# Four graph layers on one core: rounded-type mask transposes, and attention stacks by way of DRAM

## The chip, the cores and the metric

The kernel runs on one core of a Trainium2 chip. A core has a matrix engine (TensorE, PE in profiles; its weight loads are shown as PEld), three other compute engines (VectorE or DVE, ScalarE or ACT, GpSimd or POOL), a queue engine that only starts transfers here (SyncE, SP), and sixteen DMA engines. Data lie in DRAM, in the on-chip SBUF with 128 partitions, or in PSUM, into which TensorE writes. The metric is the device time of one execution in microseconds, lower is better. Three executions of the kernel before took 4090.72, 4092.49 and 4097.2 us; the median is 4092.49.

## What is computed

The input is `x` (16 graphs, 1024 nodes, 256 features) and one adjacency matrix `adj` of 1024 x 1024 integers, the same for all graphs. Four layers follow, each as `x = x + layer(relu(layernorm(x)))`. Three are graph attention layers, with 4, 1 and 1 heads; the fourth is a transformer block with 8 heads of 32 features:

```python
h = jnp.maximum(_layernorm(x, axis=-1), 0.0)
x = x + _L0_gnn_ref(h, adj, L0_gnn_W, L0_gnn_a)     # 4 heads of 64, then elu
...
# within a graph layer (L1 of them; L0 and L2 differ in heads and slopes)
h = jnp.matmul(inp, W)
e = jax.nn.leaky_relu(e_src[:, :, None] + e_dst[:, None, :], negative_slope=ALPHA)
e = jnp.where(adj[None, :, :] == 0, NEG_INF, e)
attention = jax.nn.softmax(e, axis=-1)
h_prime = jnp.matmul(attention, h)
...
# within the fourth layer
scores = jnp.einsum('fnhd,fmhd->fhnm', q, k) / jnp.sqrt(jnp.asarray(D, x.dtype))
scores = jnp.where(mask, scores, jnp.asarray(-1000000000.0, x.dtype))
attn = jax.nn.softmax(scores, axis=-1)
t = jnp.einsum('fhnm,fmhd->fnhd', attn, v).reshape(F, N, C)
x = _layernorm(x + t, ln1_g, ln1_b)
h = jax.nn.relu(jnp.einsum('fnc,cd->fnd', x, w1) + b1)
f_out = jnp.einsum('fnd,dc->fnc', h, w2) + b2
x = _layernorm(x + f_out, ln2_g, ln2_b)
```

## The kernel before

**Tiles.** A graph is eight row tiles of 128 nodes. `P` is 128, `HALF` is 512 nodes (half a graph), `TH` is 4 tiles in a half, `HG` is 4 heads in a group. The adjacency is turned once into `mask`, a byte array with the source node on partitions, which all graphs and all layers use.

**An order planned by hand.** The function `direct` emits nothing at first. It records every operation as a `Work` with an engine, an estimated duration, the buffers it reads and writes, and a rank (`rec.stream`, `KNOTS`, `LEAD`, `priority`). `Record.schedule` (L189) then plays the whole program through a model of five queues: `pe`, `act`, `dve`, `pool`, and `dma`, which is SyncE. It takes at each moment the work with the smallest rank that is ready, and emits the instructions in that order. `PASS` is the delay that it assumes before another engine can use a result; `SWITCH` times `BIAS` is the price of turning TensorE from one kind of matmul to another; `moved` and `lands` are the assumed transfer time and landing delay of a DMA; `AHEAD` and `SLACK` shape how long SyncE is held and how late a transfer is counted as there. The order on each engine is then fixed: on the chip an engine waits at an instruction whose input is late, and everything behind it waits too.

**Start.** `setup` (L661) prepares the weights of the first graph layer, then calls `neighbours` (L617) for each of the eight row blocks of `adj`. It loads 512 KB into `a32` (L621), DVE compares it with zero into `nat` (L626), TensorE turns eight 128 x 128 blocks with `transposes` (L526, instruction at L529), ACT casts them from PSUM into `mask` (L644), and DVE takes the smallest entry of each row into `least` (L653). `a32` and `nat` are both taken from the ring `r_pa` of six buffers. The layer 0 work of graphs 0 and 1 runs side by side at the start, the second in buffers lent from later stages (`lent`).

**Graph layers.** `gat` (L725): normalise (L500), transpose, project (L770), spread a row of scores over all partitions by a DRAM copy (`turn_rows` L843 writes `rd`, `spread` L852 reads it back as `row`), form weights on DVE (L868), multiply on TensorE. With four heads the products are L982 and the sums L992, in 32-column pieces; with one head it is L895.

**Attention.** For each graph, `attention` (L1082) makes keys and queries in `project` (L1125): TensorE multiplies (L1132), ACT casts to the rounded type into `hi` (L1141), DVE takes the rest into `lo` (L1144). Score matmuls in the rounded type then need a *stack* of 128 partitions for each head: four times the 32 features, as hi, hi, lo, lo for queries and hi, lo, hi, lo for keys. Sixteen transfers from SBUF to SBUF (L1154), one for each of four parts and four heads, put it together. `hi` and `lo` have one buffer each, the key stack `r_ks` one of [4, 1024], the query stack `r_qs` two of [4, 512]. There are eight such projections for each graph, 128 in all. The steps that follow are scores (L1352), exponential (L1376), mask (L1385), products (L1217); `later` places the other projections between them. For most graphs GpSimd adds weights up by accumulating transfers (L1253).

**End.** `feed` (L1398) does the two products of the transformer block (L1449), loads the rest of the sum `xr` from DRAM (L1502) and writes the output (L1574). After all planned work, a few instructions fold four checks of the value range into `flag` (L1661 to L1674); where a check fails, the slow function `general` computes everything again (L2227).

Of the kernel before, what the change touches and what calls it, by code (L numbers as in the profile page):

```python
# [22 lines left out]
P = 128  # L23
# [90 lines left out]


WEIGHT = {"pe": 1.0, "dve": 0.3}
PASS = {"pe": 0.198, "act": 0.153, "dve": 0.202, "pool": 0.13, "dma": 0.0}


class Work:  # L120
# [23 lines left out]
class Record:  # L144
# [44 lines left out]
    def schedule(self):  # L189
        for n, x in enumerate(self.work):  # L190
            x.n = n
            if x.key is None:
                x.key = priority(x)
            x.left = len(x.before)
            for y in x.before:
                y.after.append(x)
        free = dict.fromkeys(PASS, 0.0)
        queue = 0.0
        future = {e: [] for e in PASS}
        now = {e: [] for e in PASS}  # L200
        mode = "full"
        for x in self.work:
            if not x.left:
                heapq.heappush(future[x.engine], (x.ready, x.n, x))

        def opening(x):

            at, need = 0.0, {}
            for buf in x.opens:
                need[buf.ring] = need.get(buf.ring, 0) + 1  # L210
            for ring, n in need.items():
                if len(ring.free) < n:
                    return None
                at = max(at, sorted(ring.free)[n - 1][0])
            return at

        def turn(x):

            return BIAS * SWITCH.get((mode, x.modes[0]), 0.0) if x.engine == "pe" else 0.0

        def choose(e):

            at = free[e]
            while future[e] and future[e][0][0] <= at:
                x = heapq.heappop(future[e])[2]
                heapq.heappush(now[e], (x.key, x.n, x))
            best = None
            for key, n, x in now[e]:
                t = opening(x)
                if t is not None:  # L230
                    best = min(best or (1e9,), (max(at, t), key + turn(x), n, x))
            if future[e] and (best is None or future[e][0][0] < best[0]):
                for t, n, x in sorted(future[e]):
                    if opening(x) is not None:
                        t = max(t, at, opening(x))
                        best = min(best or (1e9,), (t, x.key + turn(x), n, x))
                        break
            return best

        order = []  # L240
        while True:
            choices = [(c, e) for c, e in ((choose(e), e) for e in PASS) if c]
            if not choices:
                break
            (at, _, n, x), e = min(choices, key=lambda c: c[0][0])
            if (x.key, n, x) in now[e]:
                now[e].remove((x.key, n, x))
                heapq.heapify(now[e])
            else:
                future[e].remove((x.ready, n, x))  # L250
                heapq.heapify(future[e])
            for buf in x.opens:
                _, k = heapq.heappop(buf.ring.free)
                buf.k, buf.t = k, buf.ring.tiles[k]
            us = x.us
            if e == "pe":
                us += SWITCH.get((mode, x.modes[0]), 0.0)
                mode = x.modes[1]
            x.start = at
            if x.moved:  # L260
                queue = max(at + (us if e == "pool" else 0.2), queue) + x.moved
                us = max(us, queue - at - AHEAD)
                x.pass_on = queue + x.lands + SLACK - (at + us)
            order.append(x)
            free[e] = at + us
            for buf in x.shared:
                buf.end = max(buf.end, at + us + x.pass_on)
                buf.uses.remove(x)
                if not buf.uses:
                    heapq.heappush(buf.ring.free, (buf.end, buf.k))  # L270
            for y in x.after:
                y.ready = max(y.ready, at + us + (x.pass_on if y.before[x] else 0.0))
# [10 lines left out]
KNOTS = {  # L283
    "gat0": (-6.706, -3.534, -2.307, -1.522, -2.815),
    "gat1": (0.005, 0.503, 0.618, 0.731, 0.916),
    "gat2": (0.938, 0.468, 0.637, 0.867, 1.15),
    "beside": (0.241, 1.203, 1.943, 0.54, 4.121),
    "values": (1.06, -3.362, -0.305, 3.145, 0.767),
    "steps": (1.014, 1.448, 1.59, 2.064, 1.794),
    "feed": (2.016, 2.165, 2.509, 2.154, 2.609),  # L290
    "last": (2.808, 3.335, 3.547, 5.206, 6.138),
}
BIAS = 1.225
LEAD = {"act": 9.55, "dve": -0.732}

SWITCH = {
    ("full", "col4"): 0.137,
# [30 lines left out]
def direct(ctx, tc, flag, x, adj, gat_w, gat_a, w_qkv, ln1_g, ln1_b, ln2_g, ln2_b, w1, b1, w2, b2, out):  # L328
# [33 lines left out]
    mask = const.tile([P, NT, N], U8, name="mask")  # L362

    least = const.tile([P, NT], F32, name="least")


    work = ctx.enter_context(tc.tile_pool(name="work", bufs=1))
# [53 lines left out]
    def act(us, emit, w, r):  # L421
        rec.add("act", us, emit, w, r)
# [100 lines left out]
            [b_rec],  # L523
        )

    def transposes(dst, src, n, shape=P):  # L526

        for k in range(n):
            nc.tensor.transpose(dst(k), src(k), ident[:shape, :shape])  # L529

    class Halves:

# [81 lines left out]
                [],  # L614
            )

    def neighbours(it):  # L617
        a32, nat = r_pa.new(), r_pa.new()
        a_i = a32.t.rearrange("p a n -> p (a n)").bitcast(I32)
        dma(  # L620
            1.8, 1.7, lambda: nc.sync.dma_start(a_i, adj[it * P : (it + 1) * P, :]), [a32], []  # L621
        )
        nat_f = nat.t.rearrange("p a n -> p (a n)")
        dve(
            ts_us(N),
            lambda: nc.vector.tensor_scalar(nat_f, a_i, 0.0, None, ALU.is_gt),  # L626
            [nat],
            [a32],
        )
        for j0 in range(0, NT, TH):  # L630
# [1 line left out]
            pe(  # L632
                0.109 * TH,
                lambda: transposes(
                    lambda k: g.t[:, k * P : (k + 1) * P],
                    lambda k: nat_f[:, (j0 + k) * P : (j0 + k + 1) * P],
                    TH,
                ),
                [g],
                [nat],  # L640
            )
            act(
                act_us(HALF),
# [11 lines left out]
            [a32],  # L655
        )

    def mask_of(hf):
# [423 lines left out]
    def attention(b, xt, b_mv, b_rstd):  # L1082
# [42 lines left out]
        def project(g, hf, keys, stack, at):  # L1125
# [4 lines left out]
            def product():  # L1130
# [14 lines left out]
                [lo],  # L1145
                [sc, hi],
            )
            for a in range(4):
                part = ((hi, hi, lo, lo), (hi, lo, hi, lo))[keys][a]
                for r in range(HG):  # L1150
                    dma(
                        0.3,
                        1.5,
                        lambda: nc.sync.dma_start(  # L1154
                            stack.t[a * D3 : (a + 1) * D3, r, at : at + HALF],
                            part.t[r * D3 : (r + 1) * D3, :],
                        ),
                        [stack((r, hf if keys else 0, a))],
                        [part],
                        us=0.59,  # L1160
                    )

        def values(it):
            sc = r_sc.new()
# [501 lines left out]
    good = work.tile([P, 4], F32, name="good")  # L1666
# [4 lines left out]
    nc.tensor.matmul(ps[:1, :4], ones_col, good, start=True, stop=True)  # L1671
    n_good = work.tile([1, 1], F32, name="n_good")
    nc.vector.tensor_reduce(n_good, ps[:1, :4], AX.X, ALU.add)
    nc.vector.tensor_scalar(flag, n_good, 4.0 * P - 0.5, None, ALU.is_lt)  # L1674


@with_exitstack
# [590 lines left out]
```

## Time and profile before

| | |
|---|---|
| median of three executions | 4092.49 us |
| the profiled execution | 4091.28 us, of which the span from first to last instruction is 4089.5 us |
| mean granted TensorE clock | 0.995 |
| mask transposes (L529, from `pa`) | 64 of 128 x 128, 10.9 us busy |
| score matmuls (L1352) | 2048, 717.7 us busy, mean 455 ns |
| stack transfers (L1154) | 2048 of 64 KB on SyncE's queue |
| row spreads (L852) | 184 of 256 KB on the same queue |
| accumulating transfers (L1253) | 240 of 512 KB on GpSimd's queue, median 6.0 us from issue to landing |
| all DMA traffic | 389.65 MB, of which the queue that SyncE feeds 259.36 MB (22.4% of the 16 engines' span) |

The profile is one execution, its times in microseconds from the first instruction. "PE" times overlap: matmuls are pipelined, so a mean duration of one is longer than the time between two. An arrow "<-" in a wait names the instruction that released it; in a group of instructions it stands between output and inputs.

### The profile page before, as it was taken

How to read it: one execution, taken by the hardware profiler on the slowest of the kernel's cores; microseconds unless marked ns; L12 is line 12 of the kernel's file. 1: busy time of each engine (PE TensorE's matmuls, PEld its weight loads, DVE VectorE, ACT ScalarE, POOL GpSimd, SP SyncE). 2: the span in 40 equal slices, each digit the busy share in tenths (PEclk: the TensorE clock that was granted, in tenths of full speed). 3: DMA queues.
4: the chain of work that ended last, by engine and by line, in shares of the span. 5: the costliest groups of instructions: out<-in, count | busy, mean ns of one | idle time of the engine just before them, and what ended most of it. 6: DMA issues, size and time to landing. Idle time of an engine off the chain costs nothing.

```text
span 4089.5 us, 68377 instructions
## 1 busy us (share of the span) xinstructions
PE 4023.3 (98%) x23874; PEld 2354.7 (58%) x23874; DVE 3499.0 (86%) x5994; ACT 2689.9 (66%) x6673; POOL 646.7 (16%) x631
## 2 busy tenths in 40 slices
PE   7999999999999999999999999999999999999998
PEld 3566466564655646566564665646556465665643
DVE  7768898988979799897988989889797998979866
ACT  5467676775757767576675767757577675765765
POOL 1102011121211202111121211212111011111100
PEclk9999999999999999999999999999999999999999
DMA  3024344343444324443243443434443244432441
GB/s 128 24 77 102 99 109 99 89 93 98 101 112 102 90 75 112 114 108 90 77 105 99 109 105 87 95 92 103 110 109 85 74 112 113 108 90 59 107 103 47
DMA packets 215248, 389.65 MB, mean 95 GB/s; under 512 B 45168, under 2 KB 80240, under 8 KB 214896
## 3 DMA queue, kind: packets, MB, share of 16 engines
q1 hardware_dynamic: 180336, 259.36, 22.4%
q0 software_dynamic: 34560, 125.84, 16.2%
q8 instruction: 191, 3.13, 0.3%
q14 instruction: 161, 1.32, 0.1%
HBM read 91.03 MB, written 33.95 MB: 31 GB/s over the span
## 4 chain that ended last, share of the span: by engine, by line
PE 85%; DVE 5%; ACT 4%; SPq 2%; DMA 2%; issue 1%; POOL 1%; DVEq 0%; ACTq 0%; POOLq 0%
PE bank L895 20%; PE bank L1217 14%; PE sc L1352 11%; PE bank L982 9%; PE bank L770 9%; PE bank L529 6%; PE bank L992 5%; PE bank L1449 4%; PE sc L1132 4%; PE sc L1169 2%; SPq L1154 2%; DVE pt L868 2%; DVE pa L1385 1%; POOL rstdz L466 1%; ACT waste L446 1%
## 5 line engine op out<-in xcount | busy, mean ns | idle before, releaser
L1385 DVE TENSOR_TENSOR pa<-pa,mask 128x1024 f32<-128x1024 f32 x1024 | 1221.4, 1218 | 72.4 <-ACT pa L1376 69.4
L1376 ACT ACTIVATE pa<-sc 128x512 f32<-128x512 f32 x2048 | 1098.3, 606 | 234.2 <-PE sc L1352 175.1
L868 DVE SCALAR_TENSOR_TENSOR pt<-row,e,mask 128x512 f32<-128x512 f32 x1472 | 1016.3, 744 | 62.2 <-DMA row<-rd 40.3
L895 PE MATMUL bank<-qb,pt 128*128 128x257 f32 x4096 | 942.0, 380 | 3.5 <-ACT fz L1533 3.5
L895 PEld LDWEIGHTS bank<-qb,pt 128*128 128x128 f32 x4096 | 771.3, 189 | 147.1 <-ACT pa L1376 12.6
L1352 PE MATMUL sc<-qs,ks 128*128 128x512 f32 x2048 | 717.7, 455 | 11.2 <-DMA qs<-lo 5.8
L1217 PE MATMUL bank<-pa,va 128*32 128x512 f32 x4096 | 504.8, 596 | 0.3 <-DVE pa L1385 0.2
L1352 PEld LDWEIGHTS sc<-qs,ks 128*128 128x128 f32 x2048 | 360.4, 189 | 212.3 <-ACT pa L1376 56.5
L1244 DVE TENSOR_TENSOR sums<-pa,pa 128x1024 f32<-128x1024 f32 x360 | 430.3, 1219 | 57.6 <-PE bank L1217 57.4
L982 PE MATMUL bank<-pt,qb 128*32 128x512 f32 x3840 | 468.7, 597 | 2.4 <-DVE pt L868 1.4
L770 PE MATMUL bank<-w_aug,hT 128*128 128x259 f32 (+1 forms) x1504 | 383.1, 393 | 0.5 <-ACT hT L764 0.5
L1253 POOL DMA_DIRECT2D sums<-pa x240 | 210.1, 878 | 930.5 <-DVE pa L1385 507.2
L770 PEld LDWEIGHTS bank<-w_aug,hT 128*128 128x128 f32 x1504 | 275.8, 191 | 121.1 <-ACT pa L1376 13.7
L923 ACT ACTIVATE ex<-bank,rec 128x256 f32<-128x256 f32 x256 | 122.1, 477 | 294.5 <-DVE rec L915 287.6
L982 PEld LDWEIGHTS bank<-pt,qb 128*32 128x32 f32 x3840 | 118.8, 109 | 275.9 <-issue 193.0
L1217 PEld LDWEIGHTS bank<-pa,va 128*32 128x32 f32 x4096 | 120.5, 109 | 263.0 <-issue 227.6
L992 PE MATMUL bank<-pt,e 128*32 128x512 f32 x1920 | 258.5, 592 | 0.0
L500 ACT ACTIVATE hn<-xh,mv,rstd 128x256 f32<-128x256 f32 x376 | 195.9, 592 | 93.0 <-DVE mv L490 89.1
L1132 PE MATMUL sc<-hTa,wqkv_sb 128*128 128x512 f32 x512 | 244.4, 600 | 0.1
L466 POOL TENSOR_TENSOR rstd<-rstd,neg_half 128x4 f32<-128x4 f32 x96 | 138.5, 1443 | 597.0 <-DVE rstd L458 588.3
L820 POOL TENSOR_TENSOR sum_e<-sum_e,e 128x12 f32<-128x12 f32 (+1 forms) x94 | 114.7, 1220 | 648.2 <-ACT e L781 648.1
L1141 ACT CAST hi<-sc 128x512 fp32r<-128x512 f32 x128 | 74.8, 585 | 196.4 <-PE sc L1132 72.8
(152 smaller groups left out, 4638.4 us busy)
## 6 DMA issues: line engine op xcount, KB each, us to landing
sums<-pa POOLq DMA_DIRECT2D x240, 512.0 KB, 6.0
row<-rd SPq DMA_DIRECT2D x184, 256.0 KB
ks<-hi SPq DMA_DIRECT2D x512, 64.0 KB
ks<-lo SPq DMA_DIRECT2D x512, 64.0 KB
qs<-hi SPq DMA_DIRECT2D x512, 64.0 KB
qs<-lo SPq DMA_DIRECT2D x512, 64.0 KB
xh<-in_x_dram SPq DMA_DIRECT2D x32, 512.0 KB
x<-xh SPq DMA_DIRECT2D x32, 512.0 KB
```

What stands on the lines that cost most here:

```text
L529: nc.tensor.transpose(dst(k), src(k), ident[:shape, :shape])
L770: nc.tensor.matmul(g.t[:, : C + 3 * H], hT.t[:, ct, k * P : (k + 1) * P], w_aug[l][:, ct, :], start=ct == 0, stop=ct == CT - 1,)
L868: lambda: nc.vector.scalar_tensor_tensor(pt.t, row.t, e3[:, 2, jt // TH, h, jt % TH : jt % TH + 1], mask[:, jt, hf * HALF : (hf + 1) * HAL ...
L895: nc.tensor.matmul(g.t[:, : D + 1], pts[jt].t[:, k * P : (k + 1) * P], qb[:, jt, 0, :], start=jt == 0, stop=jt == NT - 1,)
L982: nc.tensor.matmul(g.t[u * D + d : u * D + d + D3, :], qb[:, j, h + u, d : d + D3], pts[u][j - jt].t, start=j == 0, stop=j == NT - 1,)
L992: nc.tensor.matmul(gd.t[c : c + D3, :], one(jt + k, h + u).to_broadcast([P, D3]), pts[u][k].t, start=jt == 0, stop=jt == NT - 2,)
L1132: nc.tensor.matmul(sc.t, wqkv_sb[:, ct, c0 : c0 + P], hT.t[:, ct, hf * HALF : (hf + 1) * HALF], start=ct == 0, stop=ct == CT - 1,)
L1217: nc.tensor.matmul(ac.t[r * D3 : (r + 1) * D3, :], columns(r), of_head(r), start=first, stop=last,)
L1244: lambda: nc.vector.tensor_add(ss.t, p0.t, p1.t),
L1352: nc.tensor.matmul(scs[r - r0].t, ks.t[:, r, jt * P : (jt + 1) * P].bitcast(F32R), q.t[:, r, :].bitcast(F32R), start=True, stop=True,)
L1376: lambda: nc.scalar.activation(pt.t[:, v, :], sc.t, AF.Exp, scale=1.0 / math.sqrt(D3)),
L1385: lambda: nc.vector.tensor_mul(pt.t, pt.t, mask[:, jt : jt + 1, i0 : i0 + HALF].to_broadcast([P, 2, HALF]),),
```

## The change

Three edits to the work, and new constants for the planner.

1. `neighbours` writes the 0/1 tiles into the key stack (its four slots of 1024 entries, used in turn) and no longer into `r_pa`. The tiles and the identity are declared as the rounded 4-byte type for the transposes.
2. A new function `compare` turns one block of `wqkv_sb` both in the rounded type (from a copy made by a transfer) and in the plain type, and marks where the results differ. A fifth check at the end takes this into the flag.
3. `project` writes `hi` and `lo` to a DRAM buffer `hl` (three of them), and reads each of the four parts of the stack back with one transfer for all four heads.

In the planner, the rule that held SyncE until the queue was at most `AHEAD` behind is replaced by a fixed 1.35 us where it is more than 2.0 behind, and `PASS`, `SLACK`, `KNOTS`, `BIAS` and `LEAD` have other values, which changes the order of the work on all engines.

```diff
-PASS = {"pe": 0.198, "act": 0.153, "dve": 0.202, "pool": 0.13, "dma": 0.0}
+PASS = {"pe": 0.125, "act": 0.485, "dve": 0.254, "pool": 0.13, "dma": 0.0}
...
             if x.moved:
+                if e == "dma" and queue - at > BEHIND:
+                    us = max(us, HELD)
                 queue = max(at + (us if e == "pool" else 0.2), queue) + x.moved
-                us = max(us, queue - at - AHEAD)
...
-AHEAD = 3.5
-SLACK = 0.56
+BEHIND, HELD = 2.0, 1.35
+SLACK = 0.575
...
-    "gat0": (-6.706, -3.534, -2.307, -1.522, -2.815),
+    "gat0": (-7.393, -4.812, -1.57, -0.269, -4.238),
...
-    "values": (1.06, -3.362, -0.305, 3.145, 0.767),
+    "values": (1.108, -4.178, 0.405, 1.761, 0.253),
...
-    "last": (2.808, 3.335, 3.547, 5.206, 6.138),
+    "last": (2.867, 2.335, 4.13, 4.632, 5.511),
 }
-BIAS = 1.225
-LEAD = {"act": 9.55, "dve": -0.732}
+BIAS = 1.154
+LEAD = {"act": 9.736, "dve": 0.649}
...
+    ident_r = const.tile([P, P], F32R, name="ident_r")
+    nc.vector.tensor_copy(ident_r, ident)
...
+    r_hl = ring("hl", 3, [2, HALF], dram)
...
-    def neighbours(it):
-        a32, nat = r_pa.new(), r_pa.new()
+    def neighbours(it, nat):
+        a32, part = r_pa.new(), nat(it % HG)
...
-        nat_f = nat.t.rearrange("p a n -> p (a n)")
+        nat_f = nat.t[:, it % HG, :].bitcast(F32R)
...
-                    lambda k: g.t[:, k * P : (k + 1) * P],
+                    lambda k: g.t[:, k * P : (k + 1) * P].bitcast(F32R),
                     lambda k: nat_f[:, (j0 + k) * P : (j0 + k + 1) * P],
                     TH,
+                    unit=ident_r,
...
+    def compare():
+        rec.stream(0.5, (0.0, 0.0), False)
+        raw, got, g, g_r = r_qs.new(), Buf(differ, []), r_sc.new(), r_sc.new()
+        dma(1.0, 1.83, lambda: nc.sync.dma_start(raw.t[:, 0, :P], wqkv_sb[:, 0, :P]), [raw], [b_qkv])
...
+        pe(0.109 * 2, turn_both, [g, g_r], [raw, b_qkv])
+        act(act_us(HALF), lambda: nc.scalar.copy(differ, g_r.t[:, :P]), [got], [g_r])
...
+                out=differ, in0=differ, in1=g.t[:, :P], op=ALU.not_equal
...
+        nat = r_ks.new()
         for it in range(NT):
-            neighbours(it)
+            neighbours(it, nat)
...
+            hl = r_hl.new()
+            for k, part in enumerate((hi, lo)):
+                dma(0.65, 1.5, lambda: nc.sync.dma_start(hl.t[:, k, :], part.t), [hl(k)], [part])
             for a in range(4):
-                part = ((hi, hi, lo, lo), (hi, lo, hi, lo))[keys][a]
-                for r in range(HG):
-                    dma(
-                        0.3,
-                        1.5,
-                        lambda: nc.sync.dma_start(
-                            stack.t[a * D3 : (a + 1) * D3, r, at : at + HALF],
-                            part.t[r * D3 : (r + 1) * D3, :],
-                        ),
-                        [stack((r, hf if keys else 0, a))],
-                        [part],
-                        us=0.59,
-                    )
+                k = ((0, 0, 1, 1), (0, 1, 0, 1))[keys][a]
+                dma(
+                    1.0,
+                    1.83,
+                    lambda: nc.sync.dma_start(
+                        stack.t[a * D3 : (a + 1) * D3, :, at : at + HALF],
+                        hl.t[:, k, :].rearrange("(r d) n -> d r n", r=HG),
+                    ),
+                    [stack((r, hf if keys else 0, a)) for r in range(HG)],
+                    [hl(k)],
+                )
...
+    compare()
     for b in range(NB):
...
-    tot = work.tile([P, 4], F32, name="tot")
+    tot = work.tile([P, 5], F32, name="tot")
...
+    nc.vector.tensor_reduce(tot[:, 4:5], differ, AX.X, ALU.max)
...
+    nc.vector.tensor_scalar(good[:, 4:5], tot[:, 4:5], 0.5, None, ALU.is_le)
```

More of the change, by code (lines that the diff above doesn't have):

```diff
@@ L278, in schedule @@
         return order
-AHEAD = 3.5
-SLACK = 0.56
+BEHIND, HELD = 2.0, 1.35
+SLACK = 0.575
 KNOTS = {
-    "gat0": (-6.706, -3.534, -2.307, -1.522, -2.815),
-    "gat1": (0.005, 0.503, 0.618, 0.731, 0.916),
-    "gat2": (0.938, 0.468, 0.637, 0.867, 1.15),
-    "beside": (0.241, 1.203, 1.943, 0.54, 4.121),
-    "values": (1.06, -3.362, -0.305, 3.145, 0.767),
-    "steps": (1.014, 1.448, 1.59, 2.064, 1.794),
-    "feed": (2.016, 2.165, 2.509, 2.154, 2.609),
-    "last": (2.808, 3.335, 3.547, 5.206, 6.138),
-}
-BIAS = 1.225
-LEAD = {"act": 9.55, "dve": -0.732}
+    "gat0": (-7.393, -4.812, -1.57, -0.269, -4.238),
+    "gat1": (-0.136, 0.479, 0.675, 0.751, 0.909),
+    "gat2": (0.893, 0.611, 0.619, 0.795, 1.122),
+    "beside": (0.454, 2.194, 2.5, 0.836, 4.987),
+    "values": (1.108, -4.178, 0.405, 1.761, 0.253),
+    "steps": (0.862, 1.413, 1.62, 2.039, 1.779),
+    "feed": (2.044, 1.828, 1.946, 2.353, 2.551),
+    "last": (2.867, 2.335, 4.13, 4.632, 5.511),
+}
+BIAS = 1.154
+LEAD = {"act": 9.736, "dve": 0.649}
 SWITCH = {
@@ L364, in direct @@
     least = const.tile([P, NT], F32, name="least")
+    differ = const.tile([P, P], F32, name="differ")
     work = ctx.enter_context(tc.tile_pool(name="work", bufs=1))
@@ L524, in watch, with transposes @@
         )
-    def transposes(dst, src, n, shape=P):
+    def transposes(dst, src, n, unit=ident):
         for k in range(n):
-            nc.tensor.transpose(dst(k), src(k), ident[:shape, :shape])
+            nc.tensor.transpose(dst(k), src(k), unit)
     class Halves:
@@ L626, in neighbours @@
             lambda: nc.vector.tensor_scalar(nat_f, a_i, 0.0, None, ALU.is_gt),
-            [nat],
+            [part],
             [a32],
@@ L634, in neighbours @@
                 lambda: transposes(
-                    lambda k: g.t[:, k * P : (k + 1) * P],
+                    lambda k: g.t[:, k * P : (k + 1) * P].bitcast(F32R),
                     lambda k: nat_f[:, (j0 + k) * P : (j0 + k + 1) * P],
                     TH,
+                    unit=ident_r,
                 ),
                 [g],
-                [nat],
+                [part],
             )
@@ L656, in neighbours, with turn_both @@
         )
+    def compare():
[4 more added lines that the diff above has]
+            1.83,
+            lambda: nc.sync.dma_start(raw.t[:, 0, :P], wqkv_sb[:, 0, :P]),
+            [raw],
+            [b_qkv],
+        )
+        def turn_both():
+            transposes(
+                lambda k: g_r.t[:, k * P : (k + 1) * P].bitcast(F32R),
+                lambda k: raw.t[:, 0, k * P : (k + 1) * P].bitcast(F32R),
+                1,
+                unit=ident_r,
+            )
+            transposes(
+                lambda k: g.t[:, k * P : (k + 1) * P],
+                lambda k: wqkv_sb[:, 0, k * P : (k + 1) * P],
+                1,
+            )
+        pe(0.109 * 2, turn_both, [g, g_r], [raw, b_qkv])
+        act(act_us(HALF), lambda: nc.scalar.copy(differ, g_r.t[:, :P]), [got], [g_r])
+        dve(
+            tt_us(HALF),
+            lambda: nc.vector.tensor_tensor(
+                out=differ, in0=differ, in1=g.t[:, :P], op=ALU.not_equal
+            ),
+            [got],
+            [g],
+        )
     def mask_of(hf):
@@ L1147, in project @@
             )
+            hl = r_hl.new()
+            for k, part in enumerate((hi, lo)):
+                dma(0.65, 1.5, lambda: nc.sync.dma_start(hl.t[:, k, :], part.t), [hl(k)], [part])
             for a in range(4):
-                part = ((hi, hi, lo, lo), (hi, lo, hi, lo))[keys][a]
-                for r in range(HG):
-                    dma(
-                        0.3,
-                        1.5,
-                        lambda: nc.sync.dma_start(
-                            stack.t[a * D3 : (a + 1) * D3, r, at : at + HALF],
-                            part.t[r * D3 : (r + 1) * D3, :],
-                        ),
-                        [stack((r, hf if keys else 0, a))],
-                        [part],
-                        us=0.59,
-                    )
+                k = ((0, 0, 1, 1), (0, 1, 0, 1))[keys][a]
+                dma(
+                    1.0,
+                    1.83,
+                    lambda: nc.sync.dma_start(
+                        stack.t[a * D3 : (a + 1) * D3, :, at : at + HALF],
+                        hl.t[:, k, :].rearrange("(r d) n -> d r n", r=HG),
+                    ),
+                    [stack((r, hf if keys else 0, a)) for r in range(HG)],
+                    [hl(k)],
+                )
         def values(it):
@@ L1665, in direct @@
     nc.vector.tensor_reduce(tot[:, 3:4], least, AX.X, ALU.min)
-    good = work.tile([P, 4], F32, name="good")
+    nc.vector.tensor_reduce(tot[:, 4:5], differ, AX.X, ALU.max)
+    good = work.tile([P, 5], F32, name="good")
     nc.vector.tensor_scalar(good[:, :2], tot[:, :2], SAFE, None, ALU.is_le)
@@ L1669, in direct @@
     nc.vector.tensor_scalar(good[:, 3:4], tot[:, 3:4], 0.0, None, ALU.is_ge)
+    nc.vector.tensor_scalar(good[:, 4:5], tot[:, 4:5], 0.5, None, ALU.is_le)
     ps = r_bank.tiles[0]
-    nc.tensor.matmul(ps[:1, :4], ones_col, good, start=True, stop=True)
+    nc.tensor.matmul(ps[:1, :5], ones_col, good, start=True, stop=True)
     n_good = work.tile([1, 1], F32, name="n_good")
-    nc.vector.tensor_reduce(n_good, ps[:1, :4], AX.X, ALU.add)
-    nc.vector.tensor_scalar(flag, n_good, 4.0 * P - 0.5, None, ALU.is_lt)
+    nc.vector.tensor_reduce(n_good, ps[:1, :5], AX.X, ALU.add)
+    nc.vector.tensor_scalar(flag, n_good, 5.0 * P - 0.5, None, ALU.is_lt)
 @with_exitstack
```

## The prediction

> **What bounds the kernel now.** I read the page first, then busy time by stretches, then the waits of TensorE, then the last 190 us in order of time. From the page, the span, the engines and the chain that ended last (shares of the span by engine, then by line):
>
> ```profile
> span 4089.5 us, 68377 instructions
> ...
> PE 4023.3 (98%) x23874; PEld 2354.7 (58%) x23874; DVE 3499.0 (86%) x5994; ACT 2689.9 (66%) x6673; POOL 646.7 (16%) x631
> ...
> PE 85%; DVE 5%; ACT 4%; SPq 2%; DMA 2%; issue 1%; POOL 1%; DVEq 0%; ACTq 0%; POOLq 0%
> ```
>
> TensorE (PE) is busy 4023.3 of 4089.5 us and carries 85% of the chain. All its idle time is 66.2 us, 1.6% of the span; a gain must come out of that, or out of the order in which PE works. The stretches say where the idle time lies (length, then PE, PEld, DVE, ACT, POOL busy us, granted clock, DMA share, GB/s):
>
> ```profile
> 0.00:50.00 50.00, 32.74 (x202) 20.55 (x206) 38.84 (x88) 36.35 (x113) 5.39 (x12) 0.97 0.65 220
> 50.00:100.00 50.00, 41.89 (x307) 19.09 (x300) 39.85 (x82) 22.88 (x66) 5.21 (x6) 0.93 0.14 41
> ...
> 3900.00:3930.00 30.00, 23.55 (x99) 14.38 (x98) 12.25 (x35) 19.65 (x52) 5.74 (x8) 0.92 0.57 136
> 3930.00:4000.00 70.00, 66.96 (x382) 29.18 (x381) 48.62 (x55) 43.74 (x97) 1.56 (x2) 0.99 0.34 91
> 4000.00:4050.00 50.00, 50.00 (x315) 19.91 (x315) 40.45 (x47) 33.87 (x68) 1.01 (x1) 0.97 0.15 38
> 4050.00:4090.00 40.00, 23.00 (x100) 10.52 (x92) 16.93 (x47) 17.21 (x51) 4.78 (x6) 0.86 0.13 42
> ```
>
> The first 100 us hold 17.3 + 8.1 = 25.4 us of idle PE; 3900 to 4000 holds 6.5 + 3.0 = 9.5; the last stretch, which ends at 4089.5, holds 39.5 - 23.0 = 16.5. What is left, about 15 us, is spread over 3,800 us in which PE is full. The waits of PE (us in all, times, longest):
>
> ```profile
> PE bank L529 <- DVE pa L626: 12.6, 4, 11.3
> PE sc L1352 <- DMA qs<-lo: 5.8, 1, 5.8
> PE sc L1352 <- DVE lo L1144: 4.4, 4, 1.7
> ```
>
> The first is the start: PE waits 11.3 us for the first adjacency tile. The other two are attention stacks that come late, and nearly all of it is in the last batch, where no other batch fills the gap. SyncE's queue there (start, us):
>
> ```profile
> 3903.53 4.21 SPq L1154 DMA_DIRECT2D ks<-hi  x4
> 3907.79 2.50 SPq L1154 DMA_DIRECT2D ks<-lo  x4
> 3910.33 2.49 SPq L1154 DMA_DIRECT2D ks<-hi  x4
> 3912.86 3.12 SPq L1154 DMA_DIRECT2D ks<-lo  x4
> 3916.47 4.94 SPq L1154 DMA_DIRECT2D qs<-hi  x8
> 3921.51 4.97 SPq L1154 DMA_DIRECT2D qs<-lo  x8
> ```
>
> One stack costs sixteen issues at 0.62 to 0.63 us each, 10 us; keys and queries follow one another, so the first scores (L1352) start at 3926.1, 22.6 us after the first issue. The chain, in order of time, has the nearest rows for the new transfers (start, us):
>
> ```profile
> 3923.99 1.97 DMA qs<-lo
> ...
> 4069.63 2.15 DMA out_dram<-xr
> 4071.80 3.14 DMA xr<-x
> ```
>
> 64 KB from SBUF to SBUF is there 1.97 us after its issue began, 256 KB from SBUF to DRAM after 2.15, 256 KB from DRAM to SBUF after 3.14.
>
> **What the Trainium skill says.** "DMA: Bandwidth & Descriptors", section "Latency and other measured facts", puts most of a transfer's fixed cost of about 2 us in the receipt from the target memory, and calls device memory (HBM) the slowest target, worse under load. The stacks would then pay that cost twice, and the first time on the slow target. The trace agrees on the floor, but not that the write is dearer: 2.15 us for four times the bytes of the 1.97 us row. I go by the trace's two rows; the page's "worse under load" is the bad end of the range. "TensorE: Matmul & The Clock Gate", "Part 4: PE-mode transpose", gives 275 ns for a transpose in a kernel's context, mostly access latency. The trace has the same latency (278 ns mean, L529) but eight in a row take 0.87 us, 0.109 each, since they overlap. I go by 0.109.
>
> **Stacks through DRAM, at the end.** Removed: 16 issues and 1 MB for each of 128 stacks. Added: two writes and four reads of 256 KB, 1.5 MB. Where the three adjacency loads of 512 KB at 12.27 held SyncE, they went at 1.44 us each, so I estimate 0.72 us for each 256 KB. Cast to last landing: 2.15 (write) + 3.14 (first read) + 3 x 0.72 = 7.5 us, against 16 x 0.63 + 1.97 = 12.1 now. The second stack's reads queue behind the first's: about 4 x 0.72 = 2.9 us later, and up to 5 if its own write is late, so keys and queries are both there after 10.4 to 12.5 us instead of 22.6. Also, `hi` and `lo` (one buffer each) come free after one write instead of after eight issues. Of the 9.5 us of PE idle between 3900 and 4000 I take **8 off** (ends: 0 and 9.5). From 3930 to 4050 PE is full, so this reaches the end; next in line is PE itself.
>
> **The same in the body.** Between 100 and 3850 us PE lost 1.8 us to `lo`, none to the stacks: zero here, though ACT waited 33.4 us on `qs<-hi` and DVE 24.0 on `ks<-lo`; PE's other work covers those, and without that cover they would cost up to 57 us. SyncE's issue time falls from 2048 x 0.6 = 1,230 us to 768 issues at 0.33 to 0.58 (row and x rows), 250 to 450. The new wait: a read must stand on SyncE until its write has landed, about 2 us. Queued behind it are the row spreads (L852, for which DVE's weights wait), `x3` and the output. They now stand behind up to ten 0.63 us issues. I put that at zero net. DMA load: 128 x 0.5 MB more on 259.36 MB that take 22.4% is 5.8 points on a queue of that share; no bound.
>
> **Adjacency loads.** The loads start at 2.81 (three), 12.27 (three), 27.03 and 29.09, because each row block takes two of six `pa` tiles. With the 0/1 tiles in the key stack, first needed at 236 us, six loads can go at once. The gain is limited by DVE, which turns them into masks: it is idle 11.2 us of the first 50, some 6.2 of it before its first adjacency tile at 10.42. That leaves 5.0; weights (L868) start at 38.1 now. I take **3 off** (ends 0 and 6).
>
> **Mask transposes.** 64 x 0.109 = 7.0 us of PE where PE is not full. No row shows a transpose of this type. If the type halves the work it would be half, 3.5 us, hidden; a dearer one is bounded by L1352's rate, 0.232 us per 512 columns, no more than 0.109 per 128. Value: zero.
>
> **Compare.** One transfer, two transposes (0.22 us of PE and perhaps a break of 0.33), a copy and a DVE comparison under PE's cover, and two more small DVE instructions at the end, where L1663 to L1668 stand in the chain at about 0.15 each. The copy of the identity falls in DVE's first idle stretch. **0.7 on** (0.3 to 1.2).
>
> **The new order.** Every constant that ranks the work is changed, so all engines' orders change. What PE can win or lose is breaks: sixteen L1217 matmuls take 1.72 us after their like and 1.85 after others, and four L1352 take 0.93 against 1.13. So a visit to the 32-column lines (L982, L992, L1217) costs 0.13 in and 0.20 out. The timeline has about 397 visits, 131 us. A tenth more or fewer is 13 us. Nothing in the trace gives the sign: zero, ends -15 and +15.
>
> **Sum.** 4091.3 (the profiled execution; its span is 4089.5) - 8 - 3 + 0.7 = 4081.0. The median of the three runs, 4092.5, is 1.2 above it, so between 4081 and 4082; I say **4081**. A measurement of this kernel can tell about 0.2%, 8 us, from no change; 4081 is 11.5 below.
>
> **Rivals.** (a) The transfer was hidden anyway: the new order puts the last batch's gap elsewhere, or the two hops take as long as before, and the head is held by DVE. For it: only one long wait is on a stack. Against it: that wait is on the chain. 4092.5 - 3 + 0.7 = 4090. (b) The order wins: a tenth of the visits go: 4081 - 13 = 4068. (c) **Slower**: two hops under load. POOL's accumulating transfers land after 6.0 us (median, 512 KB). If each hop takes that, a stack needs 6.0 + 6.0 + 2.2 = 14.2 us, 2.1 more than 12.1; the plan is fixed, so PE stands before the first scores of a batch, which need both stacks. Half of 16 batches x 2.1 = 17, and no gain at the end: 4092.5 - 3 + 0.7 + 16.8 = 4107. It decides once cast to last landing exceeds 12.1 us. For it: DMA engines are busy 40 to 50% in the body. Against it: PE finds other work there. A worse order by a tenth gives the same size. (d) The change doesn't do what it says: if the two turns of the block differ in one bit, the flag sends everything through `general` as well. That repeats the products, 4023 - 131 = 3,890 us of PE, so at least 7,900. No run here shows whether they do; "Perfetto Trace Analysis" of the skill, section "Transposes", says that a transpose skips arithmetic, so I hold a difference unlikely.
>
> **Chances.** Forecast 58% (of which 40 faster by over 0.2%, 17 within, 1 slower), (a) 6% (5 within, 1 slower), (b) 9% faster, (c) 24% slower, (d) 3% slower. Faster 0.49, same 0.22, slower 0.29. The forecast's own range is 4068 to 4092. The range goes from 4062 (half of (b) left out, 4%) to 4110 (a third of (c), 8%, and (d), 3%).
>
> **What would show it.** Right: L1352's wait on a stack in the last batch is under 2 us and PE idle from 3900 to 4000 under 3; six adjacency loads start before 13 us and L868 starts before 36; casts don't wait on stack transfers; visits to the 32-column lines stay near 397. Wrong: PE waits on stacks in many batches (c), PE busy time away from 4023 by over 10 us (order), or a second pass after the end (d).

## The result, and the profile after

The changed kernel takes 4147.19 us (median of 4; 4140.56 to 4153.77), the kernel before 4091.6 us in the same session. The ratio is 1.0134, 95% interval 1.0119 to 1.015: **slower by 1.3%, some 55 us**, where 11 us of gain were forecast. The profiled execution has a span of 4150.9 us, 61.4 more than before. From its page, the same lines as before:

```profile
span 4150.9 us, 66181 instructions
...
PE 4036.3 (97%) x23876; PEld 2352.6 (57%) x23876; DVE 3507.1 (84%) x5998; ACT 2703.4 (65%) x6674; POOL 576.4 (14%) x631
...
PE 76%; DVE 9%; DMA 7%; ACT 4%; issue 2%; SPq 0%; POOL 0%; DVEq 0%; ACTq 0%; POOLq 0%
```

TensorE's idle time rose from 66.2 to 114.6 us, its busy time by 13.0. In the chain that ended last, DMA went from 2% to 7%, and SyncE's queue from 2% to nothing. The waits of TensorE say for what (us in all, times, longest):

```profile
PE bank L1261 <- DMA sums<-pa: 28.7, 14, 3.8
PE sc L1396 <- DMA ks<-hl: 18.2, 8, 6.4
PE bank L534 <- DVE ks L631: 12.9, 4, 11.4
PE bank L1025 <- DVE pt L911: 8.6, 4, 6.7
...
PE sc L1396 <- DMA hl<-hi: 2.4, 1, 2.4
PE sc L1396 <- DMA qs<-hl: 2.0, 1, 2.0
```

(L1261 is L1217 of the kernel before, L1396 is L1352, L534 is L529.) Score matmuls wait for a stack (three rows, 22.6 us), which the rival (c) of the forecast foresaw; but the longest row is a wait that no part of it named: the sums wait for GpSimd's accumulating transfers, once in nearly every graph. The kernel before has no row of this kind. The list of DMA issues of the page shows how long the transfers take (KB each, median us from issue to landing):

```profile
sums<-pa POOLq DMA_DIRECT2D x240, 512.0 KB, 6.0
ks<-hl SPq DMA_DIRECT2D x256, 256.0 KB, 5.7
qs<-hl SPq DMA_DIRECT2D x256, 256.0 KB, 4.4
...
hl<-hi SPq DMA_DIRECT2D x128, 256.0 KB, 5.7
```

A write of 256 KB to DRAM was put at 2.15 us in the forecast; over the whole run the median is 5.7. (The trace tells the landing of about half of the transfers to and from `hl`, in some of the other runs of two fifths; figures for them are of those. It tells all landings of the accumulating transfers.) The DMA view of 560 to 600 us, in which TensorE waits 2.4 us for a stack (until 579) and 1.0 for a sum (until 593), shows the engines (first line: busy tenths in 40 slices of 1 us; then packets, MB, share of 16 engines):

```profile
DMA  9977999700549999999999999989999999226899
...
q1 hardware_dynamic: 2804, 4.87, 46.6%
q0 software_dynamic: 867, 3.15, 41.6%
```

From 572 to 594 they are full, SyncE's queue (q1, stacks) and GpSimd's (q0, accumulating transfers) taking about equal shares. SyncE's queue in that stretch, and GpSimd's (start, us):

```profile
575.57 0.34 SPq L1193 DMA_DIRECT2D hl<-hi  x1
577.30 0.34 SPq L1193 DMA_DIRECT2D hl<-lo  x1
583.46 2.82 SPq L1199 DMA_DIRECT2D ks<-hl  x4
588.69 0.34 SPq L1193 DMA_DIRECT2D hl<-hi  x1
589.42 0.34 SPq L1193 DMA_DIRECT2D hl<-lo  x1
594.96 1.74 SPq L1199 DMA_DIRECT2D qs<-hl  x4
```

```profile
572.75 0.86 POOL L1297 DMA_DIRECT2D sums<-pa  x1 [9.98 <-DVE sums L1288]
573.86 0.86 POOL L1297 DMA_DIRECT2D sums<-pa  x1 [0.26 <-issue]
581.38 0.86 POOL L1297 DMA_DIRECT2D sums<-pa  x1 [6.66 <-DMA sums<-pa]
584.58 0.86 POOL L1297 DMA_DIRECT2D sums<-pa  x1 [2.34 <-issue]
```

The reads of a key stack start at 583.46, nearly 8 us after its first write was issued, and the third accumulating transfer starts only after 6.66 us of waiting for the one before it on the same sum.

Counted over stretches of 5 us from 300 to 3900 us, DMA engines are at 90% or more for 480 of 3,600 us before and for 695 after. The mean over all stretches rose only from 0.41 to 0.46. In the full stretches before, GpSimd's queue takes about four fifths of the engines' time and SyncE's one fifth; after, each takes about half.

One part of the loss is in no row of waits. Beside a long wait, TensorE's granted clock falls for some microseconds. At 845.41 a wait of 2.8 us for a sum ended (length, then PE, PEld, DVE, ACT, POOL busy us, granted clock, DMA share, GB/s):

```profile
845.00:850.00 5.00, 4.59 (x22) 1.16 (x23) 2.36 (x2) 2.07 (x4) 0.00 (x0) 0.66 0.49 150
850.00:855.00 5.00, 5.00 (x29) 4.41 (x28) 3.55 (x5) 2.04 (x4) 0.00 (x0) 1.00 0.75 164
```

From 300 to 3900 us the trace has eight stretches at a clock of 0.5, of 3.4 or 6.8 us, 31 us in all. Each lies beside a wait of 2.4 to 6.4 us for a stack or a sum; two waits of 2.4 and 2.5 us have none. The kernel before has no such stretch there. At half clock 31 us do the work of 15, so by estimate up to 15 us of the loss stand in TensorE's busy time.

### The profile page after: what moved, and what is told of

It is laid out like the page before. It is cut to its first block, busy times and chain, and to the rows that moved or that the text cites. A ratio compares the mean times of both kernels' runs of the same rounds, so it can differ in the third digit from the quotient of the medians.

```text
span 4150.9 us, 66181 instructions
## 1 busy us (share of the span) xinstructions
PE 4036.3 (97%) x23876; PEld 2352.6 (57%) x23876; DVE 3507.1 (84%) x5998; ACT 2703.4 (65%) x6674; POOL 576.4 (14%) x631
## 3 DMA queue, kind: packets, MB, share of 16 engines
q1 hardware_dynamic: 192768, 326.45, 27.8%
HBM read 225.25 MB, written 101.06 MB: 79 GB/s over the span
## 4 chain that ended last, share of the span: by engine, by line
PE 76%; DVE 9%; DMA 7%; ACT 4%; issue 2%; SPq 0%; POOL 0%; DVEq 0%; ACTq 0%; POOLq 0%
PE bank L938 17%; PE bank L1261 12%; PE bank L1025 10%; PE sc L1396 9%; PE bank L813 7%; PE bank L534 5%; PE bank L1493 5%; PE bank L1035 5%; DVE pt L911 4%; DMA sums<-pa 4%; PE sc L1175 4%; DVE pa L1429 3%; PE sc L1213 2%; ACT pa L1420 2%; DMA ks<-hl 1%
## 5 line engine op out<-in xcount | busy, mean ns | idle before, releaser
L1396 PE MATMUL sc<-qs,ks 128*128 128x512 f32 x2048 | 719.3, 457 | 28.2 <-DMA ks<-hl 18.2
L1261 PE MATMUL bank<-pa,va 128*32 128x512 f32 x4096 | 524.5, 603 | 0.1
L1396 PEld LDWEIGHTS sc<-qs,ks 128*128 128x128 f32 x2048 | 365.6, 189 | 251.5 <-issue 78.7
L1025 PE MATMUL bank<-pt,qb 128*32 128x512 f32 x3840 | 472.0, 597 | 8.7 <-DVE pt L911 8.6
L1025 PEld LDWEIGHTS bank<-pt,qb 128*32 128x32 f32 x3840 | 119.3, 110 | 287.9 <-issue 206.7
L1261 PEld LDWEIGHTS bank<-pa,va 128*32 128x32 f32 x4096 | 116.8, 110 | 268.8 <-issue 242.2
L1261 PE MATMUL bank<-sums,ones 128*32 128x512 f32 x1440 | 207.5, 605 | 28.7 <-DMA sums<-pa 28.7
L505 ACT ACTIVATE hn<-xh,mv,rstd 128x256 f32<-128x256 f32 x376 | 196.5, 592 | 27.8 <-DVE mv L495 20.6
```

Of the source, the lines that this page charges most:

```text
L1025: nc.tensor.matmul(g.t[u * D + d : u * D + d + D3, :], qb[:, j, h + u, d : d + D3], pts[u][j - jt].t, start=j == 0, stop=j == NT - 1,)
L1261: nc.tensor.matmul(ac.t[r * D3 : (r + 1) * D3, :], columns(r), of_head(r), start=first, stop=last,)
L1396: nc.tensor.matmul(scs[r - r0].t, ks.t[:, r, jt * P : (jt + 1) * P].bitcast(F32R), q.t[:, r, :].bitcast(F32R), start=True, stop=True,)
```

## The experiments

All times are medians; the kernel before ran beside each group and stood at 4091.2 to 4094.1 us. Ratios are to it.

**Which part.** Three parts can be set apart: the stacks' route, the planner's constants with its rule for holding SyncE, and the mask tiles with the comparison. Four kernels:

*Stacks alone:* the kernel before, and only this:

```diff
-                    dma(0.3, 1.5, lambda: nc.sync.dma_start(stack.t[...], part.t[...]), ..., us=0.59)
+            hl = r_hl.new()
+            for k, part in enumerate((hi, lo)):
+                dma(0.65, 1.5, lambda: nc.sync.dma_start(hl.t[:, k, :], part.t), [hl(k)], [part])
...
```

> The kernel before, with only the stacks by way of DRAM (planner constants and rule as before). Theory A (two DRAM hops come later than the plan assumes, and TensorE stands once or twice in each graph): it carries most of the loss, 4125 to 4150 us, with about 2 us of TensorE wait on a stack and about 2 us on an accumulated sum in each graph. Theory B (the changed constants made a worse order): 4080 to 4095 us, the last graph's stretch about 10 us shorter.

Measured: **4291.85 us**, ratio 1.0485 (1.0467 to 1.0502). Theory A had the sign and missed the size by 140 us, and its mechanism is not in the trace either: of TensorE's 160.1 us of idle time, 5.0 are waits for a stack and 2.6 for a sum. The rest is spread over many waits, most of them for DVE and ScalarE.

*Constants alone:* the kernel before with `PASS`, `KNOTS`, `SLACK`, `BIAS`, `LEAD`, `BEHIND` and `HELD` of the changed one.

> The kernel before, with only the planner's constants and its rule for holding SyncE changed. Theory A: within 10 us of 4092. Theory B: 4125 to 4150 us.

Measured: **4220.5 us**, ratio 1.0305 (1.0288 to 1.0322). Worse than the whole change, and beyond the range of theory B, which had the sign.

*The changed kernel with direct stacks:*

> The changed kernel, with only the stacks put back to sixteen direct transfers (constants, masks and comparison stay changed). Theory A: 4085 to 4105 us, no TensorE wait on a stack or an accumulated sum over 1 us in the body. Theory B: 4130 us or more.

Measured: **4230.69 us**, ratio 1.0331 (1.0314 to 1.0348), as theory B has it.

*Masks and comparison alone:*

> The kernel before, with only the mask tiles in the key stack, the rounded-type transposes and the comparison. Both theories: within 6 us of 4092; the six adjacency loads start before 13 us. A start that gains shows as TensorE reaching the first scores earlier than 259.8 us.

Measured: **4090.72 us**, ratio 0.9993 (0.9987 to 1.0). First scores at 258.9 us for 259.8. The timeline of SyncE in this run says why nothing is gained at the start: it is not the loads. SyncE starts all eight from 2.82 us on, and yet the first weights stand at 41.4 us for 38.1:

```profile
2.82 10.70 SPq L624 DMA_DIRECT2D pa<-in_adj_dram  x8
13.56 0.43 SPq L561 DMA_DIRECT2D w_aug<-in_L_gnn_W_dram  x1
```

Behind them stands everything else that DVE needs (`w_aug` and so on), so DVE does the masks earlier and the rest later. The last thing before the first weights is the comparison, which waits for ScalarE's copy:

```profile
DVE differ L691 <- ACT differ L688: 3.0, 1, 3.0
```

So masks and comparison cost nothing in the old order. (With the new constants and direct stacks, the run with them took 10 us more than the one without, 4230.7 for 4220.5; what they cost in the changed kernel was not measured.) Neither theory stands as put: constants and route are not separate amounts. Each alone costs 128 to 199 us, together 55. The ranks of either kernel suit one set of transfers. In both mismatched orders TensorE's *busy* time rises too: 4126.6 us with the stacks alone, 4096.7 with the constants alone, for 4023.3. In the timeline the visits to the 32-column lines are 482 and 524 for 397. At 0.33 us each that is 28 and 42 us; the rest of the rise is not accounted for by them.

**What holds the changed order.** From here on, each step stays where it was, and only what the steps issue is changed.

*The same order, stacks moved directly:*

```diff
-                dma(0.65, 1.5, lambda: nc.sync.dma_start(hl.t[:, k, :], part.t), [hl(k)], [part])
+                dma(0.65, 1.5, lambda: None, [hl(k)], [part])
...
-                    lambda: nc.sync.dma_start(stack.t[...], hl.t[:, k, :].rearrange(...)),
+                    lambda: four(stack.t[a * D3 : (a + 1) * D3, :, at : at + HALF], mine[k]),
```

> The changed kernel with the order of every planned step kept to the letter, but the stacks moved physically by direct transfers: the two writes issue nothing, each of the four reads issues four 64 KB transfers from hi or lo. Where a later cast stands ahead of such a transfer in the order, it carries the later data, so part of the stacks holds other values; the flag's threshold is set so that the second pass never runs. Theory A (at a given order the two hops and their traffic make the once-a-graph waits): 4095 to 4115 us, waits on sums<-pa under 8 us in all and on a stack under 8. Theory B (the order itself is the loss): 4135 us or more, with TensorE full or waiting elsewhere.

Measured: **4440.96 us**, ratio 1.0853 (1.0837 to 1.087). The time lies in the range of theory B, 4135 us or more, but so far up that the order alone need not be the reason. This order leaves no time for sixteen issues, nor for `hi` and `lo` being held until the last of them. Waits of this kernel (all engines):

```profile
DVE lo L1197 <- DMA qs<-lo: 190.0, 19, 13.8
...
PE bank L538 <- DVE ota L1370: 139.9, 14, 10.8
...
DVE lo L1197 <- DMA ks<-lo: 95.6, 12, 9.0
```

DVE stands up to 13.8 us at `lo` until the transfers out of it are done, and TensorE then stands behind DVE. So the run does not tell the two theories apart; it shows that the new order does use what the DRAM route frees, SyncE and the two buffers.

*Half the bytes:* the same order, transfers and waits, half the columns in each transfer of a stack; the other half of each stack stays zero.

> The changed kernel, same order, same transfers and same waits, but each write and read of a stack moves only the first half of the columns (128 KB instead of 256); the other half of the stacks stays zero; the second pass never runs. If the loss is traffic (DMA engines full while a graph's first stacks and the accumulating transfers meet): 4100 to 4120 us, hl writes land in under 4 us. If it is the second hop as such (latency, the wait of the read for the write): within 12 us of 4147.

Measured: **4060.59 us**, ratio 0.9924 (0.9909 to 0.994). Its longest waits of TensorE:

```profile
PE bank L534 <- DVE ks L631: 12.9, 4, 11.3
PE bank L1032 <- DVE pt L918: 6.7, 1, 6.7
PE bank L534 <- DVE yT L1538: 5.9, 2, 2.9
```

No stack and no accumulated sum is among them, though there are still two hops and the reads still wait for the writes. Packets on SyncE's queue are as many as in the changed kernel (192,768); their share of the engines fell from 27.8% to 18.2%. The time is 40 us below what the traffic theory said: half the bytes take away more than the half megabyte that the change had added.

*No accumulating transfers* (the sums then lack terms):

```diff
-                            lambda: nc.gpsimd.dma_start(ss.t, pt.t, accum_op=ALU.add),
+                            lambda: None,
```

> The changed kernel, same order, without GpSimd's accumulating transfers (the row sums then lack terms; the second pass never runs). If the loss is two kinds of transfer meeting on the DMA engines: hl writes land in about 2 us as in the last graph, the wait on a stack goes to under 5 us in all, and the time to 4090 to 4110 us. If it is the second hop as such: only the 28.7 us of waits on sums<-pa can go, 4115 to 4125 us, and the stack waits of about 20 us stay.

Measured: **4063.75 us**, ratio 0.9928 (0.9913 to 0.9943). The stacks move all their 1.5 MB, and their waits fall from 18.2 + 2.4 + 2.0 to 4.1 us:

```profile
PE sc L1396 <- DMA hl<-hi: 2.6, 1, 2.6
...
PE sc L1396 <- DMA qs<-hl: 1.5, 1, 1.5
```

One expectation failed in part: the writes of `lo` land after 2.1 us in the median (5.6 before), but those of `hi` still after 5.6. All transfers to and from `hl` together have 4.7; the slowest fell from 10.1 to 7.9 us. The time is 26 us below the range of the traffic theory. The whole gain is 83 us where the rows of both waits hold 51. Most of the rest lies in TensorE's busy time, which fell from 4036.3 to 4006.6 us, by 29.7. Up to about half of that is the clock: from 300 to 3900 us this run has no stretch at 0.5, and its slowest L1261 matmul there takes 618 ns, against 1063 in the changed kernel. What is left fits short waits inside the L1261 groups, which leave no gap because matmuls overlap. The run with two parts, below, has them without the clock: no L1271 matmul over 617 ns from 300 to 3900 us, and yet the two rows of these groups hold 516.3 + 202.4 us, against 506.9 + 190.6 here.

*Fewer bytes in steps:* three parts of the stack are read back, then two; the terms of the others are left out.

```diff
+                if a >= PARTS:
+                    dma(1.0, 1.83, lambda: None, [stack(...) ...], [hl(k)])
+                    continue
```

> The changed kernel, same order, with three of the four parts of each stack read back: the product of the two small remainders (lo times lo) is left out of the scores, the fourth part of the query stacks stays zero. A stack moves 1.25 MB instead of 1.5. If bytes on full DMA engines are the loss (4147 at 1.5 MB, 4061 at 0.75): about 4118 us if it goes evenly with the bytes, nearer 4070 if it is a threshold. If the number of hops is the loss: 4140 to 4150 us.

> As the run with three parts, but only two read back (the low part of the queries is left out of the scores): 1.0 MB for each stack, the same bytes as sixteen direct transfers. Bytes: 4065 to 4095 us. Hops: 4135 us or more.

Measured: **4092.63 us** with three parts, ratio 1.0 (0.9992 to 1.0008), and **4076.77 us** with two, ratio 0.9962 (0.9948 to 0.9977). Three parts lie between the even and the threshold case. The waits of TensorE on sums with three parts:

```profile
PE bank L1271 <- DMA sums<-pa: 12.8, 9, 3.3
```

and with two:

```profile
PE bank L1271 <- DMA sums<-pa: 3.3, 5, 1.2
```

Together, all in the changed order (the third column counts stretches of 5 us from 300 to 3900 us; the fourth is of those transfers to and from `hl` whose landing the trace tells; the profiled execution at 1.25 MB took 4100.3 us, 8 over its median):

| MB for each stack | us | of 3,600 us, DMA at 90% or more | slowest landing, us | slowest accumulation, us |
|---|---|---|---|---|
| 1.5 | 4147.2 | 695 | 10.1 | 12.6 |
| 1.25 | 4092.6 | 565 | 8.4 | 10.0 |
| 1.0 | 4076.8 | 470 | 8.5 | 9.2 |
| 0.75 | 4060.6 | 400 | 7.5 | 7.7 |
| 1.5, no accumulation | 4063.8 | 170 | 7.9 | none |

The last quarter of a megabyte costs 55 us, each of the two below it 16. The rows were not made in the same way: 1.25 and 1.0 MB have fewer reads, 0.75 has all of them at half size.

*Halving elsewhere.* The same cut for the stacks alone, and for the kernel before:

> The kernel before with only the stacks by way of DRAM (4292 us), and each transfer of a stack cut to half the columns as in the changed kernel's run of that kind; the second pass never runs. If its 199 us are an order that does not fit the new transfers (the old ranks), halving the bytes takes away little: 4220 us or more. If they are traffic too: under 4150 us.

> The kernel before, same order, with each of the sixteen direct transfers of a stack cut to half the columns (0.5 MB for a stack instead of 1.0; the other half stays zero, the second pass never runs). If the kernel before is held by DMA traffic as the changed one is: 4065 to 4080 us. If traffic matters only above what it moves (1.0 MB): 4085 to 4093 us, and the 4061 us of the changed order at half bytes is then a better order.

Measured: **4246.35 us** for the first (ratio 1.0373, 1.0358 to 1.0388): of its 199 us, some 46 go with the bytes, and some 153 stay with the old ranks. **4084.32 us** for the second (ratio 0.9981, 0.9973 to 0.9988): just under the range of its second expectation. The kernel before gains 7 us from half the bytes, the changed one 87. So traffic is the matter of the changed kernel, and once it is small, the new order together with its route is the better one by 4084.3 - 4060.6 = 24 us; which of the two gives it was not set apart.

**The end.** Stacks by way of DRAM in the last graph alone, the rest as before:

```diff
+            if b == NB - 1:
+                hl = r_hl.new()
...
+                return
```

> The kernel before, with the stacks of the last graph alone by way of DRAM. If the shorter stretch after the last graph's first projection (190.8 us before, 179.6 us changed) comes from the stacks: 4081 to 4086 us. If it comes from the other ranks of the last graph's work: within 4 us of 4092.

Measured: **4088.19 us**, ratio 0.9989 (0.9982 to 0.9995): outside the first expectation and at the edge of the second. From the last graph's first projection to the end it takes 186.9 us, the kernel before 190.8, the changed one 179.6. The route is worth about 4 us there; the other 7 of the changed kernel would then come with its other ranks, which wasn't tried by itself. This is the fastest version here that computes everything.

## Why the prediction was wrong

**The failed step: "5.8 points on a queue of that share; no bound".** With it the body was put at zero. The traffic was sized right (q1's share rose from 22.4% to 27.8%, 5.4 points), and judged by its mean over the span. But a graph's first stacks meet GpSimd's accumulating transfers, which by themselves took most of the engines' time in the 480 of 3,600 us that were at 90% or more before the change. There half a megabyte more means that something lands later, stack or sum; 480 us became 695, and the kernel lost 55 us instead of gaining 11. The run with half the bytes and the one without accumulation gain 87 and 83 us on the changed kernel, more than the whole loss; with 1.0 MB, the bytes of the direct stacks, it is 70. The two hops and the read's wait for the write stay in all three, so by themselves they aren't the cause.

**The duration of the write.** 2.15 us came from a row of the tail, where the engines are nearly idle (a share of 0.13 from 4050 to 4090 us). Over the whole run the median is 5.7. The page "DMA: Bandwidth & Descriptors" of the Trainium skill, "Latency and other measured facts", says that the fixed cost grows with the load on the memory; the forecast kept that for the bad end. The direction agrees. But accumulation from SBUF to SBUF slows as well: its median stays at 6.0, its slowest goes from 8.9 to 12.6 us. And without accumulation the same 225.25 MB are read from DRAM and the same 101.06 written, while stacks are waited for 4.1 us instead of 22.6. So the load on DRAM alone is not it. What both kinds share, the sixteen engines and the on-chip memory at their ends, was not set apart further.

**Rival (c) had the kind of failure and half of the place.** It gave 4107, with 17 us of score matmuls waiting for stacks; they wait 22.6 us. From the end of the cast to the landing of a stack's fourth read the trace has 14.8 us in the median (96 stacks of 128), close to (c)'s 14.2. But 12.1 us, the point where (c) decides, was a time of the last graph: over the whole kernel before, the last of the sixteen issues ends 12.8 us after the cast in the median, to which its landing is added. So a stack by way of DRAM is hardly later than a direct one; that the new plan counts on it sooner would fit, but was not tested. And (c) looked only at the stack: the sums hold 28.7 us, and the half clock and the short hidden waits come on top. Who else uses the engines in that stretch was not asked.

**"The new order: zero, ends -15 and +15" was wrong in kind.** Ranks and transfers belong together: the new ranks cost 128 us with the old transfers, the old ranks 199 us with the new ones. The forecast's sign of a worse order, busy time off by over 10 us, did come (13.0), but it pointed to the wrong thing: the same order with half the bytes is 21 us less busy than the kernel before. Counting visits to the 32-column lines was no measure either, for that run has 423 visits, 26 more than before.

**The last graph: 8 forecast, 11.2 seen** between its first projection and the end, of which the route by itself gave about 4. That the total comes near the forecast is therefore in part luck. The mechanism held: no stack is waited for as long as 5.8 us there; the longest is 2.4.

**Adjacency loads: 3 forecast, 0.8 measured** at the first scores (masks alone), and nothing in the time. The loads did start at once. DVE was the limit, as the bound of 5.0 said: it had the masks earlier and the rest later, and then stood 3.0 us for the comparison. **Mask transposes: zero**, as forecast; the 64 are busy 9.4 us in the rounded type (masks alone), 10.9 before. **Comparison: 0.7 forecast.** There was no second pass, so (d) fell. It had a price that the forecast didn't see, a wait of DVE in the start with the weights queued behind it. In the changed kernel it is longer than with the masks alone:

```profile
DVE differ L693 <- ACT differ L690: 4.7, 1, 4.7
```

TensorE then stood 6.7 us for the first weights (L1025). First scores come at 260.1 us in spite of it, 259.8 before, so it didn't reach the end.

**SyncE in the body: zero, and no run speaks against it.** The queue left the chain (2% to 0%). But a read stands longer than the forecast's 2 us: two waits for `hl` in the stretch from 560 to 600 us took 10.9 us, the longer one 5.8.

## What to carry to other kernels

Judge an added transfer by the busiest stretch that it falls into, not by the mean share of the DMA engines, and list who else moves data there: the one who pays may be a transfer that wasn't touched. Take a transfer's duration from a row under the same load. In a kernel whose order is planned from assumed durations, constants and mechanism form one change; tested apart, each looks far worse than both, and neither number may be booked as its share.

## What the runs showed of the hardware that was not expected

The cost of bytes has a knee in this order, a point from which it is steeper: from 0.75 to 1.25 MB for a stack each quarter costs 16 us, the next one 55. And a wait of TensorE can cost more than its idle time. Beside eight waits of 2.4 to 6.4 us the clock was at 0.5 for 3.4 or 6.8 us, in which an L1261 matmul took up to 1063 ns for 592 to 618; the profile counts that as busy. The runs in which these waits are gone (half the bytes, two parts, no accumulation) have no such stretch from 300 to 3900 us. That the wait brings the slow stretch on was not tested by itself.
